# A two-layer RWKV and retention block with routed experts: each scatter and gather of GpSimd tied to an instruction of VectorE, and the scatters moved back

## The chip, the cores and the metric

The kernel runs on one core of a Trainium2 chip. The time is the device time of one execution, in microseconds (us). The engines are TensorE (PE, with its weight loads PEld), VectorE (DVE), ScalarE (ACT), GpSimd (POOL) and SyncE (SP); each takes its instructions in order, and waits at an instruction whose semaphores are not there yet.

## What is computed

The input x is 4 x 1024 tokens of 256 numbers. Two attention layers alternate with the same feed-forward layer, each behind a layer norm and added to x:

```python
x = x + attn_a(layernorm(x))   # RWKV: r, v, k = x @ W; a recurrence over the 1024 tokens; sigmoid(r) * wkv @ W_out
x = x + ffn(layernorm(x))
x = x + attn_b(layernorm(x))   # retention: (q k^T * gamma^(i-j)) v, normed by head, gated, @ wo
x = x + ffn(layernorm(x))

# ffn: 64 experts of 64 hidden units, 4 for each token, and a shared expert for all
_, topk_idx = top_k(x @ router_w + router_bias, 4)
routed = sum over the 4 of score * (silu(x @ wg[e]) * (x @ wu[e])) @ wd[e]
shared = (silu(x @ swg) * (x @ swu)) @ swd
return routed + shared
```

## The kernel before

**Tiling.** The 4096 tokens are cut into 8 segments of 512, numbered 0 to 7, two to a batch row (SPB is 2). A segment is 4 tiles (TT) of 128 tokens. The residual x stays in SBUF for the whole kernel.

**The feed-forward layer** (class `Ffn`, instances f1 and f2) runs in three steps.

- *Route* a segment: norm it (L210, ScalarE, writes the rows `xn_f`), form the router's logits, pick four experts, and count for each token and choice the row `to_f` of a DRAM array `sent` in which it is to lie, so that each expert's tokens stand together in pages of 128 rows. Then *send*: 16 indirect DMAs (L411, issued by GpSimd; 4 tiles x 4 choices) scatter 128 rows each. Beside it runs the *shared* expert: products on TensorE (L435, L448), SiLU on ScalarE (L440), the product with the gate on VectorE (L441), and the sum onto x (L453).
- *Routed* experts: 83 pairs of pages, in order. For each pair SP loads the rows (`rx_f`, L508) and the weights of the pair's experts (`rw_f`, L510); TensorE transposes (L520), VectorE copies (L524, `rxT_f`), TensorE multiplies (L532), ScalarE and VectorE form SiLU and product (L537, L540), TensorE goes down (L551), and ScalarE issues the DMA of the results to a DRAM array `made` (L558). All pages depend on all sends: SP's first load waits until the last one has landed.
- *Gather*: for each tile of 128 tokens, four *fetches* (L580, indirect DMAs of GpSimd) bring its four rows of `made` into a buffer `gy_f`, and four instructions of VectorE (L591) add them onto x, weighted. The adds are due 7 pairs behind the fetches (LAG).

**Order.** Each part of the work is a list of steps. `track(steps, lo, hi)` gives the steps due times spread evenly from lo to hi, and `merge` traces the steps of several tracks by due time. A scheduler then sets the order within each engine; an instruction put under `keep_in_program_order` keeps its place among the others traced. Before the change the adds have this, the sends and fetches do not.

**Stages.** Stage 1 (0 to 385 us) runs the RWKV attention of all eight segments beside the routing and shared expert of f1. The middle (385 to about 1160 us) runs the routed pages and gathers of f1, then stage 2, the retention of four batch rows (`batch(b)`, with the decayed product `pm` at L1009 on VectorE), beside the routing of f2's segments 0 to 5. Its ending routes segments 6 and 7 and runs, as filling, the shared expert of segments 2, 3 and 4 (`fill`, due from 1 to SPB). The second layer (1160 to the end) runs the routed pages, gathers and stores of f2, and the rest of the shared expert.

**Buffers.** The normed rows `xn_f` lie in rotating buffers: 4 in stage 1 (`rows = ffn.rows = (pa, 4)`), 3 in stage 2 (`f2.rows = (pt, 3)`). A norm waits until the sends that read its buffer's earlier contents are done.

Of the kernel before, what the change touches and what calls it, by code (L numbers as in the profile page):

```python
# [10 lines left out]
F32 = mybir.dt.float32  # L11
# [10 lines left out]
P = 128  # L22
D = 256
KC = D // P
SEG = 512
TT = SEG // P
E = 64
F = 64
TOPK = 4
# [19 lines left out]
def track(steps, lo, hi):  # L49

    return [(lo + (hi - lo) * n / len(steps), step) for n, step in enumerate(steps)]
# [9 lines left out]
def hybrid_kernel(ctx: ExitStack, tc: tile.TileContext, a: dict, out: bass.AP):  # L61
    nc = tc.nc
# [10 lines left out]


    USUAL = [(max(E + 2 + 10 * i, (i + 1) * SEG * TOPK // P + E // 2 + 6) + 1) // 2 for i in range(NSEG)]

    def seg_dram(t, i):
        b, s = divmod(i, SPB)
# [148 lines left out]
    class Ffn:  # L227
# [17 lines left out]
        def route(self, i):  # L245
# [159 lines left out]
                nc.vector.tensor_mul(out=wv, in0=wv, in1=bc(sm, 2, TOPK))  # L405
                self.pick[i] = dict(to=to, w=w)

            def send(t):
                for k in range(TOPK):
                    c = t * TOPK + k  # L410
                    ins = nc.gpsimd.indirect_dma_start(  # L411
                        out=rows_sent[: pairs_until(i) * 2 * P, :],
                        out_offset=bass.IndirectOffsetOnAxis(ap=st["to"][:, c : c + 1], axis=0),
                        in_=st["xn"][:, t, :], in_offset=None,
                    )
                    group = f"sends_{self.name}"
                    tc.declare_no_dep(
                        ins.ins, group=group, reason="each token has a row of its own"
                    )
                    tc.add_to_no_dep_group(group, ins.ins)  # L420

            return [norm, logits, pick, rank, place, weigh], [lambda t=t: send(t) for t in range(TT)]

        def shared(self, i):
            nm = f"{self.name}{i}"
            st = {}

            def up(c):
                if c == 0:
                    st["h"] = self.pool.tile([P, NS, SEG], F32, tag="sh", bufs=1, name=f"sh_{nm}")  # L430
                s = slice(c * P, (c + 1) * P)
                g, u = bank("A", f"g_{nm}_{c}"), bank("A", f"u_{nm}_{c}")
                for ps, w in ((g, self.weights[0]), (u, self.weights[1])):
                    for k in range(KC):
                        nc.tensor.matmul(  # L435
                            ps, lhsT=w[:, k, s], rhs=self.xnT[i][:, k, :],
                            start=(k == 0), stop=(k == KC - 1),
                        )
                h = st["h"][:, c, :]
                nc.scalar.activation(out=h, in_=g, func=AF.Silu)  # L440
                nc.vector.tensor_mul(out=h, in0=u, in1=h)  # L441

            def down(q):
                o = bank("C", f"o_{nm}_{q}", [P, 2, D])
                for t in range(2):
                    s = slice((2 * q + t) * P, (2 * q + t + 1) * P)
                    for c in range(NS):
                        nc.tensor.matmul(  # L448
                            o[:, t, :], lhsT=st["h"][:, c, s], rhs=self.weights[2][:, c, :],
                            start=(c == 0), stop=(c == NS - 1),  # L450
                        )
                xt = xs[i][:, 2 * q : 2 * q + 2, :]
                nc.vector.tensor_add(out=xt, in0=o, in1=xt)  # L453

            return [lambda c=c: up(c) for c in range(NS)] + [
                lambda q=q: down(q) for q in range(TT // 2)
            ]
# [38 lines left out]
        def routed(self, pool, until):  # L496
# [18 lines left out]
            def up(p):  # L515
                nm, s = f"{self.name}{p}", st[p]
                tp = bank("B", f"rt_{nm}", [P, KC, 2, P])
                for j in range(2):
                    for k in range(KC):
                        nc.tensor.transpose(  # L520
                            tp[:, k, j, :], s["x"][:, j, k * P : (k + 1) * P], ident
                        )
                xT = pool.tile([P, KC, 2, P], F32, tag="rxT", bufs=2, name=f"rxT_{nm}")
                nc.vector.tensor_copy(out=xT, in_=tp)  # L524
                s["xT"] = xT

            def mid(p):
                nm, s = f"{self.name}{p}", st[p]
                gu = bank("A", f"rg_{nm}", [P, 2, P])
                for j in range(2):  # L530
                    for k in range(KC):
                        nc.tensor.matmul(  # L532
                            gu[:, j, :], lhsT=s["w"][:, j, k * 2 * F : (k + 1) * 2 * F],
                            rhs=s["xT"][:, k, j, :], start=(k == 0), stop=(k == KC - 1),
                        )
                act = pool.tile([P, 2, P], F32, tag="rs", bufs=2, name=f"rs_{nm}")
                nc.scalar.activation(out=act[F:], in_=gu[:F], func=AF.Silu)  # L537

                h = pool.tile([P, 2, P], F32, tag="rh", bufs=2, name=f"rh_{nm}")
                nc.vector.tensor_mul(out=h[:F], in0=gu[F:], in1=act[F:])  # L540
                nc.scalar.copy(out=h[F:], in_=h[:F])  # L541
                s["h"] = h

# [25 lines left out]
        def gather(self, i, pool, until):  # L569


            nm, s = f"{self.name}{i}", self.pick[i]
            ready = [min(until(NSEG - 1), until(i) + PACE * t) for t in range(TT)]
            got = {}

            def fetch(t):
                y = pool.tile([P, TOPK, D], F32, tag="gy", bufs=self.deep[2], name=f"gy_{nm}_{t}")
                for k in range(TOPK):
                    c = t * TOPK + k
                    nc.gpsimd.indirect_dma_start(  # L580
                        out=y[:, k, :], out_offset=None,
                        in_=rows_made[: ready[t] * 2 * P, :],
                        in_offset=bass.IndirectOffsetOnAxis(ap=s["to"][:, c : c + 1], axis=0),
                    )
                got[t] = y

            def add(t):
                for k in range(TOPK):
                    c = t * TOPK + k

                    tc.keep_in_program_order(nc.vector.scalar_tensor_tensor(  # L591
                        out=xs[i][:, t, :], in0=got[t][:, k, :], scalar=s["w"][:, c : c + 1],
                        in1=xs[i][:, t, :], op0=ALU.mult, op1=ALU.add,
                    ))

            return [lambda t=t: fetch(t) for t in range(TT)], [lambda t=t: add(t) for t in range(TT)]

        def gathers(self, pool, until):

# [7 lines left out]

    def stage_1(ctx: ExitStack, ffn, pf):
        pa = ctx.enter_context(tc.tile_pool(name="pa", bufs=1))
        rows = ffn.rows = (pa, 4)  # L610

        rvk = pa.tile([P, KC, 3 * D], F32, name="rvk")
        wout = pa.tile([P, KC, D], F32, name="wout")
# [27 lines left out]
        def wkv(i):  # L641
# [37 lines left out]
            def weights(hf):  # L679
# [9 lines left out]
                    out=o[:, 1:], data0=w_t[:, hf : hf + 1].to_broadcast([P, SEG]), data1=k,  # L689
                    initial=o[:, 0:1], op0=ALU.add, op1=ALU.max,  # L690
                )
                nc.vector.tensor_sub(out=k, in0=k, in1=o[:, :SEG])
                a2, b2, c = (work(n, hf) for n in ("a2", "b2", "c"))
                nc.scalar.activation(out=a2, in_=k, func=AF.Relu, bias=w_neg[:, hf : hf + 1])
                nc.scalar.activation(
# [10 lines left out]
            def sums(hf):  # L706
# [10 lines left out]
                nc.vector.tensor_add(out=den, in0=c, in1=q[:, :SEG])  # L717
                nc.scalar.activation(out=inv, in_=den, func=AF.Ln)
                nc.scalar.activation(out=inv, in_=inv, func=AF.Exp, scale=-1.0)
                nc.vector.tensor_mul(out=b2, in0=b2, in1=v)  # L720
                nc.vector.tensor_tensor_scan(
                    out=p[:, 1:], data0=a2, data1=b2, initial=p[:, 0:1], op0=ALU.mult, op1=ALU.add
                )
                y = pa.tile([P, SEG], F32, tag=f"y{hf}", bufs=2, name=f"y_{i}_{hf}")
                num = a2
                nc.vector.tensor_mul(out=num, in0=c, in1=v)
                nc.vector.tensor_add(out=num, in0=num, in1=p[:, :SEG])
                nc.vector.scalar_tensor_tensor(
                    out=num, in0=s["r"], scalar=1.0, in1=num, op0=ALU.add, op1=ALU.mult
# [2 lines left out]
                nc.vector.scalar_tensor_tensor(  # L732
                    out=inv, in0=den, scalar=2.0, in1=inv, op0=ALU.subtract, op1=ALU.mult
                )
                nc.vector.scalar_tensor_tensor(
                    out=y, in0=num, scalar=-0.5, in1=inv, op0=ALU.mult, op1=ALU.mult
                )
                st[f"y{hf}"] = y

            def output(h):  # L740
# [35 lines left out]
        for i in range(NSEG):  # L776
# [8 lines left out]
            tracks.append(track([lambda f=output, h=h: f(h) for h in range(TT // 2)], at + 1.6, at + 1.7))  # L785
            choose, send = ffn.route(i)
            tracks.append(track(choose, at + 1.8, at + 3.3))
            tracks.append(track(send, at + 3.3, at + 3.4))

            behind = max(0, i - NSEG + 4)  # L790
            tracks.append(track(ffn.shared(i), at + 2.2 + 2 * behind, at + 4.2 + 2 * behind))
# [4 lines left out]
    def stage_2(ctx: ExitStack):  # L796
# [117 lines left out]
        def batch(b):  # L914
# [91 lines left out]

            def decayed(j, g):
                pm = pw.tile([P, KC, 2, CH], F32, tag="pm", bufs=5, name=f"pm_{b}_{j}_{g}")
                nc.vector.tensor_mul(  # L1009
                    out=pm, in0=ch[j]["sc"][g],  # L1010
                    in1=decay.rearrange("p (k g b) n -> p g k b n", k=KC, b=2)[:, g],
                )
                ch[j]["pm"][g] = pm

            def values(j):
# [107 lines left out]
    def first_layer(until):  # L1123
# [14 lines left out]
        with right("turned") as pt:  # L1138
# [13 lines left out]
            beside = [[s for s in batches if s[0] >= cut]]  # L1152
            for i in range(last):
                choose, send = f2.route(i)
                beside.append(track(choose + send, at[i], at[i + 1]))
                if i < BESIDE:
                    beside.append(track(f2.shared(i), at[i + 1], at[i + 3]))
            merge(*beside)
# [3 lines left out]
            for n, i in enumerate(range(last, NSEG)):  # L1162
                choose, send = f2.route(i)
                ending += [
                    track(choose[:2], 0, 0.2), track(choose[2:], n + 0.2, n + 1),
                    track(send, SPB, SPB + 1),
                ]
            fill = []
            for i in range(BESIDE, BESIDE + FILL):
# [89 lines left out]
```

## Time and profile before

| | |
|---|---|
| time, median of 9 runs | 1475.5 us (1472.83 to 1479.4) |
| the profiled execution's own time | 1477.4 us |
| its span | 1475.7 us |
| mean granted clock of TensorE | 0.956 |
| busy: PE, DVE, ACT, POOL | 1279.3, 999.5, 747.6, 518.4 us |
| sends (L411) | 256, mean 1046 ns, from 88.0 to 1166.4 us |
| fetches (L580) | 256, mean 968 ns |

Times of single events are microseconds from the start of the span, in one profiled execution. In a row of the groups stand the line, the engine, the operation, its output and inputs and the count; then busy time and mean ns of one; then the idle time of the engine just before such instructions, and what ended most of it. In a timeline a row is start, duration, engine, line, operation, and in square brackets the idle time ahead of it and what released it. In the list of waits the three numbers are us in all, times, and the longest.

### The profile page before, as it was taken

What the parts mean: (1) busy time and instruction counts of PE and PEld (TensorE: products, weight loads), DVE (VectorE), ACT (ScalarE), POOL (GpSimd) and SP (SyncE); (2) the same over time, 40 slices, a digit from 0 to 9 for tenths busy, and PEclk for the clock granted to TensorE, in tenths of its full rate; (3) what the DMA queues carried; (4) which work ended last, traced back from release to release, by engine and by line L of the source; (5) the groups of instructions that cost most, each with busy time, mean ns of one, the idle gap of its engine ahead of it and who ended that gap; (6) DMA issues with size and microseconds to landing.
All of it is one profiled execution on the core that took longest, in us unless ns stands there. A gap on an engine that the chain in (4) does not pass through costs nothing. (4 is left out here: it accounts for less than half of the span.)

```text
span 1475.7 us, 23662 instructions
## 1 busy us (share of the span) xinstructions
PE 1279.3 (87%) x7872; PEld 897.5 (61%) x7872; DVE 999.5 (68%) x2490; ACT 747.6 (51%) x1433; POOL 518.4 (35%) x536
## 2 busy tenths in 40 slices
PE   6789999999388778999998997999998699998982
PEld 2455545655266666777776664667755477866752
DVE  6998989997255456677767775577659155576654
ACT  7988888953044444557544463254253044444440
POOL 0042344455300244424234105363143400277655
PEclk9999999999699999999999898999999899999997
DMA  9975921113599975666552011121011499999994
GB/s 351 401 229 78 290 93 58 58 54 100 169 323 332 325 254 162 198 204 210 169 169 89 25 48 67 48 92 46 30 58 43 139 318 321 353 389 390 371 316 120
DMA packets 192298, 276.27 MB, mean 187 GB/s; under 512 B 53795, under 2 KB 119718, under 8 KB 192166
## 3 DMA queue, kind: packets, MB, share of 16 engines
q1 hardware_dynamic: 143686, 163.98, 35.0%
q0 software_dynamic: 24576, 67.14, 13.7%
q10 hardware_dynamic: 23904, 43.53, 7.8%
q8 instruction: 65, 1.06, 0.3%
q14 instruction: 67, 0.55, 0.1%
HBM read 166.05 MB, written 121.11 MB: 195 GB/s over the span
## 5 line engine op out<-in xcount | busy, mean ns | idle before, releaser
L411 POOL DMA_INDIRECT sent<-xn_f,to_f x256 | 267.7, 1046 | 463.6 <-issue 217.9
L580 POOL DMA_INDIRECT gy_f<-made,to_f x256 | 247.8, 968 | 481.2 <-DMA made<-ry_f 149.4
L532 PE MATMUL rg_f<-rxT_f,rw_f 128*128 128x128 f32 x1328 | 188.2, 285 | 16.0 <-DVE rxT_f L524 7.4
L532 PEld LDWEIGHTS rg_f<-rxT_f,rw_f 128*128 128x128 f32 x1328 | 166.8, 196 | 28.0 <-DVE rxT_f L524 20.3
L537 ACT ACTIVATE rs_f<-rg_f 64x256 f32<-64x256 f32 x166 | 62.2, 375 | 230.7 <-PE rg_f L532 204.9
L524 DVE COPY rxT_f<-rt_f 128x512 f32<-128x512 f32 x166 | 114.3, 689 | 80.6 <-PE rt_f L520 78.7
L520 PE MATMUL rt_f<-ident,rx_f 128*128 128x128 f32 x664 | 108.1, 286 | 67.4 <-DMA rx_f<-sent 57.8
L551 PE MATMUL rp_f<-rw_f,rh_f 64*128 64x128 f32 x1328 | 133.3, 299 | 4.2 <-DVE rh_f L540 2.1
L591 DVE SCALAR_TENSOR_TENSOR x<-gy_f,w_f,x 128x256 f32<-128x256 f32 x256 | 122.5, 481 | 14.2 <-DMA gy_f<-made,to_f 9.5
L520 PEld LDWEIGHTS rt_f<-ident,rx_f 128*128 128x128 f32 x664 | 74.2, 144 | 94.9 <-issue 47.5
L557 ACT COPY ry_f<-rp_f 128x256 f32<-128x256 f32 x266 | 93.1, 373 | 74.8 <-PE rp_f L551 48.1
L448 PE MATMUL o_f<-f_swd,sh_f 128*128 128x256 f32 x512 | 123.0, 387 | 8.6 <-DVE sh_f L441 4.2
L435 PE MATMUL g_f<-xnT_f,f_swg 128*128 128x512 f32 x256 | 128.2, 616 | 1.3 <-DVE pm L1009 0.8
L435 PE MATMUL u_f<-xnT_f,f_swu 128*128 128x512 f32 x256 | 122.1, 596 | 0.7 <-DVE sh_f L441 0.7
L551 PEld LDWEIGHTS rp_f<-rw_f,rh_f 64*128 64x128 f32 x1328 | 99.4, 188 | 30.6 <-issue 8.4
L448 PEld LDWEIGHTS o_f<-f_swd,sh_f 128*128 128x128 f32 x512 | 95.3, 192 | 30.8 <-issue 6.7
L540 DVE TENSOR_TENSOR rh_f<-rg_f,rs_f 64x256 f32<-64x256 f32 x166 | 70.7, 426 | 63.8 <-ACT rs_f L537 60.8
L1009 DVE TENSOR_TENSOR pm<-sc,decay 128x512 f32<-128x512 f32 x128 | 84.5, 683 | 24.2 <-PE sc L1001 19.2
L655 PE MATMUL rvk<-xnT_a,rvk 128*128 128x512 f32 x192 | 91.2, 621 | 7.9 <-DVE xnT_a L224 7.5
L541 ACT COPY rh_f<-rh_f 64x256 f32<-64x256 f32 x166 | 66.9, 403 | 40.2 <-DVE rh_f L540 31.6
L441 DVE TENSOR_TENSOR sh_f<-u_f,sh_f 128x512 f32<-128x512 f32 x64 | 43.6, 683 | 61.3 <-PE u_f L435 44.5
L440 ACT ACTIVATE sh_f<-g_f 128x512 f32<-128x512 f32 x64 | 37.8, 596 | 89.7 <-PE g_f L435 52.7
(238 smaller groups left out, 2184.3 us busy)
## 6 DMA issues: line engine op xcount, KB each, us to landing
rw_f<-wx SPq DMA_DIRECT2D x332, 192.0 KB
rx_f<-sent SPq DMA_DIRECT2D x166, 256.0 KB
made<-ry_f ACTq DMA_DIRECT2D x166, 256.0 KB
sent<-zeros SPq DMA_DIRECT2D x7, 2048.0 KB
sent<-zeros SPq DMA_DIRECT2D x1, 10240.0 KB
x<-in_x_dram SPq DMA_DIRECT2D x8, 512.0 KB
wx<-in_wg_dram SPq DMA_DIRECT2D x2, 2048.0 KB
sent<-xn_f,to_f POOLq DMA_INDIRECT x256, 2.4
```

The lines of the kernel that those rows point to most:

```text
L411: ins = nc.gpsimd.indirect_dma_start(out=rows_sent[: pairs_until(i) * 2 * P, :], out_offset=bass.IndirectOffsetOnAxis(ap=st["to"][:, c : c ...
L435: nc.tensor.matmul(ps, lhsT=w[:, k, s], rhs=self.xnT[i][:, k, :], start=(k == 0), stop=(k == KC - 1),)
L448: nc.tensor.matmul(o[:, t, :], lhsT=st["h"][:, c, s], rhs=self.weights[2][:, c, :], start=(c == 0), stop=(c == NS - 1),)
L520: nc.tensor.transpose(tp[:, k, j, :], s["x"][:, j, k * P : (k + 1) * P], ident)
L524: nc.vector.tensor_copy(out=xT, in_=tp)
L532: nc.tensor.matmul(gu[:, j, :], lhsT=s["w"][:, j, k * 2 * F : (k + 1) * 2 * F], rhs=s["xT"][:, k, j, :], start=(k == 0), stop=(k == KC - 1),)
L551: nc.tensor.matmul(yp[:, j, :], lhsT=s["h"][r, j, :], rhs=s["w"][r, j, WD:], start=True, stop=True,)
L557: copy(out=y[:, :, c * P : (c + 1) * P], in_=yp)
L580: nc.gpsimd.indirect_dma_start(out=y[:, k, :], out_offset=None, in_=rows_made[: ready[t] * 2 * P, :], in_offset=bass.IndirectOffsetOnAxis( ...
L591: tc.keep_in_program_order(nc.vector.scalar_tensor_tensor(out=xs[i][:, t, :], in0=got[t][:, k, :], scalar=s["w"][:, c : c + 1], in1=xs[i][ ...
L655: nc.tensor.matmul(ps, lhsT=rvk[:, k, lo : lo + P], rhs=st["xnT"][:, k, :], start=(k == 0), stop=(k == KC - 1),)
L1009: nc.vector.tensor_mul(out=pm, in0=ch[j]["sc"][g], in1=decay.rearrange("p (k g b) n -> p g k b n", k=KC, b=2)[:, g],)
```

## The change

A helper `beat` notes the latest of some instructions of VectorE as they are traced: the shared expert's product (L441), the routed copy and product (L524, L540), four steps of the RWKV sums (L692, L720, L726, L735) and the decayed product (L1009). A helper `on_beat` keeps a send or fetch in program order and adds a wait for the beat noted last, if that lies in the same block of the program. All sends and all fetches get it. A segment's sends become 8 steps of two in place of 4 of four, its fetches 16 steps of one in place of 4 of four. Three due times of sends move: in stage 1 from 3.3..3.4 to 3.6..5.4 steps after the segment's, in stage 2 behind the choice by one segment's time, in the ending from SPB..SPB + 1 to SPB + n/2..SPB + n/2 + 0.5 (n is 0 for segment 6 and 1 for segment 7). In stage 1 the rows get five buffers.

```diff
+    beats = {}
+
+    def beat(ins):
+
+        beats.update(name=ins.ins.name, bb=nc.cur_bb)
+
+    def on_beat(ins):
+
+        tc.keep_in_program_order(ins)
+        if beats.get("bb") is nc.cur_bb:
+            tc.add_manual_dep(
+                ins.ins, beats["name"],
+                mybir.DependencyInfo(mybir.DependencyClass.Sync, mybir.DependencyReason.DATA),
+                reason="on_beat",
+            )
...
-            def send(t):
-                for k in range(TOPK):
+            def send(t, half):
+                for k in range(half * TOPK // 2, (half + 1) * TOPK // 2):
...
+                    on_beat(ins)
+
+            return [norm, logits, pick, rank, place, weigh], [
+                lambda t=t, h=h: send(t, h) for t in range(TT) for h in range(2)
+            ]
...
-                nc.vector.tensor_mul(out=h, in0=u, in1=h)
+                beat(nc.vector.tensor_mul(out=h, in0=u, in1=h))
...
+            def fetch(t, k):
+                if k == 0:
+                    got[t] = pool.tile(
+                        [P, TOPK, D], F32, tag="gy", bufs=self.deep[2], name=f"gy_{nm}_{t}"
+                    )
+                c = t * TOPK + k
+                ins = nc.gpsimd.indirect_dma_start(
+                    out=got[t][:, k, :], out_offset=None,
+                    in_=rows_made[: ready[t] * 2 * P, :],
+                    in_offset=bass.IndirectOffsetOnAxis(ap=s["to"][:, c : c + 1], axis=0),
+                )
+                on_beat(ins)
...
-        rows = ffn.rows = (pa, 4)
+        rows = ffn.rows = (pa, 5)
...
-            tracks.append(track(send, at + 3.3, at + 3.4))
+            tracks.append(track(send, at + 3.6, at + 5.4))
...
-                beside.append(track(choose + send, at[i], at[i + 1]))
+                beside.append(track(choose, at[i], at[i + 1]))
+                beside.append(track(send, at[i + 1] + 0.5, 2 * at[i + 1] - at[i] + 0.5))
...
-                    track(send, SPB, SPB + 1),
+                    track(send, SPB + n / 2, SPB + n / 2 + 0.5),
```

## The prediction

> **What bounds the kernel now.** I read the page first, for busy shares and the costliest groups, then the waits of each engine, then the timelines of GpSimd, VectorE, ScalarE and TensorE around the places where a send or fetch ends a wait.
>
> ```profile
> span 1475.7 us, 23662 instructions
> ...
> PE 1279.3 (87%) x7872; PEld 897.5 (61%) x7872; DVE 999.5 (68%) x2490; ACT 747.6 (51%) x1433; POOL 518.4 (35%) x536
> ...
> L411 POOL DMA_INDIRECT sent<-xn_f,to_f x256 | 267.7, 1046 | 463.6 <-issue 217.9
> L580 POOL DMA_INDIRECT gy_f<-made,to_f x256 | 247.8, 968 | 481.2 <-DMA made<-ry_f 149.4
> ```
>
> TensorE is busy 87% and is the bound in the middle; the second layer runs with the DMA engines busy 0.96 to 1.05 of the time. GpSimd is busy 35%: its sends and fetches cost time only where another engine waits for them. The page's groups give the unit: a send takes 1.05 us, a fetch 0.97, and the timeline shows 0.30 idle between two, so 32 sends in a row need 41 us. The waits of each engine hold two places where sends end a long idle time: SP's first load of the second layer's routed rows, and one norm on ScalarE.
>
> (The columns are us in total, times, longest.)
>
> ```profile
> SPq L508 <- DMA sent<-xn_f,to_f: 37.3, 1, 37.3
> ```
>
> ```profile
> ACT xn_f L210 <- DMA sent<-xn_f,to_f: 17.9, 1, 17.9
> ```
>
> The boundary before the second layer, in GpSimd's timeline and then VectorE's:
>
> ```profile
> 1094.52 0.96 POOL L411 DMA_INDIRECT sent<-xn_f,to_f  x1 [0.30 <-issue]
> 1126.33 1.10 POOL L411 DMA_INDIRECT sent<-xn_f,to_f  x1 [30.86 <-ACT w_f L401]
> 1127.73 0.96 POOL L411 DMA_INDIRECT sent<-xn_f,to_f  x1 [0.30 <-issue]
> ...
> 1166.41 0.96 POOL L411 DMA_INDIRECT sent<-xn_f,to_f  x1 [0.30 <-issue]
> ```
>
> ```profile
> 1145.39 0.69 DVE L441 TENSOR_TENSOR sh_f<-u_f,sh_f 128x512 f32<-128x512 f32 x1 [2.25 <-PE u_f L435]
> 1148.83 0.69 DVE L441 TENSOR_TENSOR sh_f<-u_f,sh_f 128x512 f32<-128x512 f32 x1 [2.74 <-PE u_f L435]
> 1152.21 0.69 DVE L453 TENSOR_TENSOR x<-o_f,x 128x512 f32<-128x512 f32 x1 [2.69 <-PE o_f L448]
> 1156.72 0.69 DVE L453 TENSOR_TENSOR x<-o_f,x 128x512 f32<-128x512 f32 x1 [3.81 <-PE o_f L448]
> 1160.25 0.69 DVE L441 TENSOR_TENSOR sh_f<-u_f,sh_f 128x512 f32<-128x512 f32 x1 [2.84 <-PE u_f L435]
> 1172.75 0.69 DVE L524 COPY rxT_f<-rt_f 128x512 f32<-128x512 f32 x1 [11.81 <-PE rt_f L520]
> ```
>
> The last 32 sends (segments 6 and 7) run from 1126.33 to 1167.4 without a gap, beside the shared expert of segment 4 (the 'fill'). They begin as soon as segment 6's destinations exist; nothing orders them against the fill. The fill ends, VectorE goes idle for 11.81 us, and the first routed page follows the last send. So here **the sends are the path**: what delays the first of them delays the kernel.
>
> **The change, part by part.**
>
> *The ending's sends.* Due times put the last 32 sends half a step behind all of the fill, and each now waits for the last beat traced ahead of it. In the built order that beat is, for all 32, the fill's last product, the row at 1148.83, ending at 1149.52. VectorE's last 70 instructions of this stage stand in the same order in both programs, and so do TensorE's, SP's and GpSimd's of the whole second layer, so nothing fills the hole. A send starts 0.7 to 0.8 us after what it waited for (segment 6's destinations were done at 1125.6, the send began at 1126.33), so the first starts at 1150.3: 24.0 later. Queued behind it on GpSimd are the other 31, behind those on SP the page loads of the whole layer, whose first load of rows waits for all of them, and behind that TensorE. The stream loses a few lengthened sends (1.10, 1.49, 1.14 in this row of 32), at most 0.9 us, as VectorE and TensorE are idle under its second half. **+23.3** (22.5 to 24.0).
>
> *Sends of segments 0 to 5 of the second layer*, one segment later. The one wait of ScalarE above is norm L210 of segment 3, whose buffer (3 in rotation) still holds segment 0's rows:
>
> ```profile
> 885.54 0.60 ACT L440 ACTIVATE sh_f<-g_f 128x512 f32<-128x512 f32 x1
> 904.06 0.60 ACT L210 ACTIVATE xn_f<-x,off_f,rstd_f 128x256 f32<-128x256 f32 x1 [17.92 <-DMA sent<-xn_f,to_f]
> ```
>
> ScalarE stands still from 886.14 to 904.06, TensorE runs dry 10.7 us later (896.8) and idles 8.18 us, with 2.3 us more in short gaps after it: 10.5 us lost. In the changed order that norm stands some 20 ScalarE instructions later, behind two more products of segment 0's shared expert, which ScalarE reaches at 929.4 by the clock of before. Segment 0's last sends wait for beats at 925.4 (a decayed product, L1009) and 927.8 (L441); eight are queued behind the first: 8 x 1.265 = 10.1 us, and 2.4 to land, from 925.4 + 0.7, so 938 at the latest. ScalarE waits about 8 us in place of 17.9, and TensorE lasted 10.7 us before. By that row the loss goes entirely (-10.5); if the cover is thinner there, all of it stays (0). I take **-7**, nearer to the full gain, as 8 is under 10.7. The next two such norms have their buffers at 974 (needed 984.6) and 994 (needed 1000): no stall, but the second has 6 us only; if sends slip by 10, it costs 4. Segment 5's sends now end near 1101 and not 1095.5, ahead of segment 6's at 1126: free.
>
> *Sends of the first layer.* Segments 0 to 4 move up to 20 us later (segment 0 from 105 to 124). Their readers are the buffers, now five: the next use of segment 0's has about 65 us of slack. The last three segments' sends are set by their own destinations, and their beats are long past:
>
> ```profile
> 362.14 1.31 POOL L411 DMA_INDIRECT sent<-xn_f,to_f  x1 [5.46 <-ACT w_f L401]
> ...
> 382.89 0.96 POOL L411 DMA_INDIRECT sent<-xn_f,to_f  x1 [0.30 <-DMA sent<-xn_f,to_f]
> ```
>
> The order of all five engines in this block is the same. The last send of this layer stays where it is: **0** (-1 to +1).
>
> *Fetches of the first layer* (501 to 817). Most beats lie at or before the fetch's present start. The late ones are late by 5 to 12 us: segment 3's second group from 606-610 to 613-620, segment 5's first from 691.7 to 704.4, its third from 722.1 to 733.3, segment 6's second from 757.5 to 768, its last from 785.3 to 794.6. Behind them on GpSimd wait only other fetches; VectorE's adds (L591) come later: 653.7, 733.3, 765.3, 797.6, 803.8. The tightest is the last: 794.6 + 0.8 + 0.96 and 4.8 to land is 801.2, 2.6 us ahead. The last segment's 16 fetches keep their times. **0** (0 to +4: the tightest group late by all of its landing).
>
> *Fetches of the second layer.* Each beat lies 0.9 to 8 us before the fetch's present start, and GpSimd runs them back to back. In the tail (1443 to 1467) the beats are at or before 1443.1, the first fetch at 1447.7. A second condition may cost a wait instruction of 17 ns (the shortest of GpSimd's in the trace): 16 x 0.017 = **+0.3** (0 to 1).
>
> *Contention.* A reason for beats would be that a transfer is described faster in VectorE's shadow. Sends above the usual 0.96 us add up to 256 x 0.086 = 22 us, all GpSimd's, and of these under 1 us lies at each boundary. VectorE pays nothing: L441 took 0.69 us beside a send and without one. The Trainium skill (SBUF — State Buffer, "Who interferes with whom") says that GpSimd can't write descriptors while VectorE holds the shared port in a two-port mode, so a transfer of 620 ns can take 3100. The trace agrees in kind (minimum 954 ns, longest 4488) but not in weight: the median is 960. By the rule's ratio freeing the sends would gain hundreds of us; by the rows the path gains 1 at most.
>
> **Sum:** 23.3 - 7 + 0.3 = +16.6. On the profiled execution's own time, 1477.4 (its span 1475.7 and 1.7 around it), 1494.0; that execution lies 1.9 above the median of nine, 1475.5, so on the median **1492**.
>
> **The rivals.**
>
> *Stage 2 chokes as well* (0.12). The pacing holds rows longer, three buffers turn over one segment later, and ScalarE's wait comes back at segments 3, 4 and 5. For it: the 6 us margin above. Against: a later need as well. Price: the 10.5 stay and up to 10 are added: 23.3 + 0 to 10, 1499 to 1509.
>
> *Faster* (0.07). ScalarE's stall goes whole (-10.5) and the boundary is covered: this needs the 32 sends to start no later than about 1126 + 10, that is the fill done 14 us sooner than it now is. For it: with the stall gone the chain into the fill might move ahead of segment 6's routing. Against: the fill's order behind the routing is the same on VectorE. It decides from a boundary loss under 10.5; full price 1475.5 - 10.5 = 1465.
>
> *The change does not bind* (0.04). Beats already past at most places, and a stall gain cancelling part of the boundary: 1472 to 1479. Against: for 32 sends the beat is 23 us away.
>
> **How the numbers follow.** My forecast (1485 to 1498) has 0.77, the choking 0.12, faster 0.07, no effect 0.04. The range takes the sum's ends, 1475.5 + 22.5 - 10.5 = 1487 with some room below, and the choking's lower half: 1482 to 1505. About 0.2%, 3 us, is what a measurement can tell from no change; so faster 0.07, same 0.04, slower 0.89.
>
> **What would show it.** GpSimd's timeline: the first of the last 32 sends about 24 us behind segment 6's destinations and under 1 us behind the fill's last product; VectorE's gap before the first L524 copy of the second layer at about 35 us and not 11.81; SP's wait for sends longer by about 23; ScalarE's longest wait at L210 under 10 us, and TensorE without the 8.18 gap. I am wrong if the second layer begins at its old distance from the routing, if L210 still waits 18, or if adds (L591) wait for fetches between 650 and 810.

## The result, and the profile after

| | before | after |
|---|---|---|
| median | 1478.31 us (62 runs) | 1494.05 us (20 runs) |
| ratio of after to before, 95% interval | | 1.0112, 1.0098 to 1.0127 |
| the profiled execution, span | 1475.7 us | 1498.3 us |
| granted clock of TensorE in it | 0.956 | 0.943 |

The change makes the kernel 1.12% slower, 16.6 us of 1478.31 (14.5 to 18.8 by the interval; the medians themselves lie 15.7 apart). The profiled spans lie 22.6 us apart; why that is more than 16.6 is said below, with the length of the second layer. Lines of the changed kernel are numbered anew: the send is L427, the fetch L601, the shared product L460, the routed copy L543, the norm L226. The kernels of the experiments have numbers of their own; the names tell which instruction a row is (`sh_f` on VectorE the shared product, `rxT_f` the routed copy, `xn_f` on ScalarE the norm).

The page of the changed kernel, the span and the two groups of GpSimd:

```profile
span 1498.3 us, 23758 instructions
...
L427 POOL DMA_INDIRECT sent<-xn_f,to_f x256 | 272.3, 1064 | 475.6 <-issue 179.9
L601 POOL DMA_INDIRECT gy_f<-made,to_f x256 | 249.8, 976 | 485.1 <-DMA made<-ry_f 128.1
```

A send did not get shorter (1046 ns before, 1064 after), nor a fetch. The loss is at the boundary before the second layer. GpSimd's timeline there (start, duration, then the idle time ahead and its releaser), and VectorE's:

```profile
1093.38 0.96 POOL L427 DMA_INDIRECT sent<-xn_f,to_f  x1 [0.30 <-issue]
1141.87 0.95 POOL L427 DMA_INDIRECT sent<-xn_f,to_f  x1 [47.53 <-DVE sh_f L460]
1143.13 0.96 POOL L427 DMA_INDIRECT sent<-xn_f,to_f  x1 [0.30 <-issue]
...
1181.03 0.96 POOL L427 DMA_INDIRECT sent<-xn_f,to_f  x1 [0.30 <-issue]
```

```profile
1117.50 0.16 DVE L409 TENSOR_TENSOR to_f<-to_f,to_pg_f 128x16 uint32<-128x16 uint32 x1
...
1140.91 0.69 DVE L460 TENSOR_TENSOR sh_f<-u_f,sh_f 128x512 f32<-128x512 f32 x1 [2.74 <-PE u_f L454]
...
1152.33 0.69 DVE L460 TENSOR_TENSOR sh_f<-u_f,sh_f 128x512 f32<-128x512 f32 x1 [2.84 <-PE u_f L454]
1187.38 0.69 DVE L543 COPY rxT_f<-rt_f 128x512 f32<-128x512 f32 x1 [34.37 <-PE rt_f L539]
```

The first of the last 32 sends names the product as its releaser: GpSimd was idle 47.53 us, and segment 6's destinations (`to_f`, the first row of VectorE) had been done at 1117.7. The row at 1140.91 is the fill's last product, that at 1152.33 the first of segment 5. The hole ahead of the first routed copy is 34.37 us and was 11.81. From the fill's last product to that copy it takes 46.5 us and took 23.9: **+22.6**. SP's wait for sends grew from 37.3 to 60.1:

```profile
SPq L527 <- DMA sent<-xn_f,to_f: 60.1, 1, 60.1
```

The product itself comes 7.9 us sooner than before (1140.91 for 1148.83). Of these, 1.8 lie ahead of the first layer's last routed copy (776.14 for 777.92), and 6.1 in stage 2, where ScalarE waits less. ScalarE's timeline, with the one row that answers to the wait of 17.92:

```profile
908.94 0.60 ACT L459 ACTIVATE sh_f<-g_f 128x512 f32<-128x512 f32 x1 [2.84 <-PE g_f L454]
916.13 2.07 ACT L226 ACTIVATE xn_f<-x,off_f,rstd_f 128x256 f32<-128x256 f32 x4 [6.59 <-DMA sent<-xn_f,to_f]
```

### The profile page after: what moved, and what is told of

The parts are those of the page before. It is cut to its first block, busy times and chain, and to the rows that moved or that the text cites. A ratio compares the mean times of both kernels' runs of the same rounds, so it can differ in the third digit from the quotient of the medians.

```text
span 1498.3 us, 23758 instructions
## 1 busy us (share of the span) xinstructions
PE 1291.0 (86%) x7872; PEld 910.9 (61%) x7872; DVE 1000.5 (67%) x2491; ACT 745.5 (50%) x1431; POOL 525.1 (35%) x536
## 5 line engine op out<-in xcount | busy, mean ns | idle before, releaser
L427 POOL DMA_INDIRECT sent<-xn_f,to_f x256 | 272.3, 1064 | 475.6 <-issue 179.9
L601 POOL DMA_INDIRECT gy_f<-made,to_f x256 | 249.8, 976 | 485.1 <-DMA made<-ry_f 128.1
L543 DVE COPY rxT_f<-rt_f 128x512 f32<-128x512 f32 x166 | 114.3, 689 | 86.3 <-PE rt_f L539 84.2
L570 PE MATMUL rp_f<-rw_f,rh_f 64*128 64x128 f32 x1328 | 139.6, 302 | 5.1 <-DVE rh_f L559 3.3
L467 PE MATMUL o_f<-f_swd,sh_f 128*128 128x256 f32 x512 | 128.7, 400 | 8.7 <-DVE sh_f L460 4.5
L570 PEld LDWEIGHTS rp_f<-rw_f,rh_f 64*128 64x128 f32 x1328 | 105.5, 191 | 32.2 <-ACT ry_f L576 8.0
L467 PEld LDWEIGHTS o_f<-f_swd,sh_f 128*128 128x128 f32 x512 | 99.0, 199 | 33.7 <-issue 8.3
L1032 DVE TENSOR_TENSOR pm<-sc,decay 128x512 f32<-128x512 f32 x128 | 84.4, 683 | 22.6 <-PE sc L1024 19.2
L454 PEld LDWEIGHTS u_f<-xnT_f,f_swu 128*128 128x128 f32 x256 | 48.2, 191 | 56.9 <-issue 51.8
```

The lines of the kernel that those rows point to most:

```text
L427: ins = nc.gpsimd.indirect_dma_start(out=rows_sent[: pairs_until(i) * 2 * P, :], out_offset=bass.IndirectOffsetOnAxis(ap=st["to"][:, c : c ...
L454: nc.tensor.matmul(ps, lhsT=w[:, k, s], rhs=self.xnT[i][:, k, :], start=(k == 0), stop=(k == KC - 1),)
L467: nc.tensor.matmul(o[:, t, :], lhsT=st["h"][:, c, s], rhs=self.weights[2][:, c, :], start=(c == 0), stop=(c == NS - 1),)
L543: beat(nc.vector.tensor_copy(out=xT, in_=tp))
L570: nc.tensor.matmul(yp[:, j, :], lhsT=s["h"][r, j, :], rhs=s["w"][r, j, WD:], start=True, stop=True,)
L601: ins = nc.gpsimd.indirect_dma_start(out=got[t][:, k, :], out_offset=None, in_=rows_made[: ready[t] * 2 * P, :], in_offset=bass.IndirectOf ...
```

## The experiments

Two theories were set against each other. **Mine:** the boundary costs 23 us and the later norm of stage 2 gives back about 7; everything else is free. **The rival:** the waits cost something in many places (fetches, tail, stage 2), and the boundary is partly covered by the 12 us hole that was there. The ratios of the experiments are to the kernel before, in runs beside it on one chip.

### The last sends freed

```diff
-                    on_beat(ins)
+                    if not (self.name == "f2_" and i >= NSEG - SPB):
+                        on_beat(ins)
...
-                    track(send, SPB + n / 2, SPB + n / 2 + 0.5),
+                    track(send, SPB, SPB + 1),
```

> The changed kernel, but the last 32 sends (segments 6 and 7 of the second layer) neither kept in program order nor made to wait for a beat, and due as before. The order of the instructions on all five engines is that of the changed kernel; only this wait is gone. Theory (the boundary is the loss, stage 2 is a gain): the first of the 32 sends starts at segment 6's destinations again, VectorE's gap before the first routed copy of the second layer is about 12 us in place of 34, the time falls by 22 to 24 us below the changed kernel and ends 5 to 8 us below the kernel before. Rival (the paced sends and fetches cost time as well): it stays at or above the kernel before, ratio 1.000 to 1.006.

Measured: 1472.68 us, ratio 0.9963 (0.9940 to 0.9987). GpSimd's timeline of this kernel, then VectorE's:

```profile
1118.75 1.10 POOL L427 DMA_INDIRECT sent<-xn_f,to_f  x1 [24.06 <-ACT w_f L417]
```

```profile
1141.25 0.69 DVE L461 TENSOR_TENSOR sh_f<-u_f,sh_f 128x512 f32<-128x512 f32 x1 [2.74 <-PE u_f L455]
...
1165.26 0.69 DVE L544 COPY rxT_f<-rt_f 128x512 f32<-128x512 f32 x1 [11.89 <-PE rt_f L540]
```

The first send starts at the destinations again, the hole is 11.89, and from product to copy it takes 24.0 us as before. All other waits of the change are still in this kernel, and it is faster than the one before by 0.37%, 5.5 us. So the rest of the change is a gain, and the boundary is the loss.

### The last sends alone held back

The helpers `beat` and `on_beat` are those of the change; due times and everything else are as in the kernel before.

```diff
+                    if (self.name == "f2_" and i >= NSEG - SPB):
+                        on_beat(ins)
...
-                nc.vector.tensor_mul(out=h, in0=u, in1=h)
+                beat(nc.vector.tensor_mul(out=h, in0=u, in1=h))
```

> The kernel before, with one part of the change: the last 32 sends wait for the last product of the filling shared expert (L441). Order on PE, DVE, ACT and SP as in the kernel before. Theory: the boundary alone costs 22 to 24 us, ratio 1.015 to 1.016, VectorE's gap before the first routed copy near 35 us, and ScalarE's wait of 17.9 us in stage 2 is still there. Rival (the second layer also runs slower in the changed kernel for another reason, such as the fetches' waits): the boundary costs clearly less than the change and the gain of stage 2 together, ratio under 1.012.

Measured: 1502.52 us, ratio 1.0156 (1.0125 to 1.0187), that is 23.1 us of 1477.7. ScalarE's wait of 17.9 us is still there. VectorE's timeline:

```profile
1148.36 0.69 DVE L459 TENSOR_TENSOR sh_f<-u_f,sh_f 128x512 f32<-128x512 f32 x1 [2.74 <-PE u_f L453]
...
1194.73 0.69 DVE L542 COPY rxT_f<-rt_f 128x512 f32<-128x512 f32 x1 [34.26 <-PE rt_f L538]
```

The hole is that of the changed kernel (34.26), the product is where it was before (1148.36). One part of the change, in the kernel before, makes the whole loss.

### The last sends held back half as long

The beat is now only the first of the four products of segment 4's shared expert.

```diff
-                beat(nc.vector.tensor_mul(out=h, in0=u, in1=h))
+                ins = nc.vector.tensor_mul(out=h, in0=u, in1=h)
+                if i == BESIDE + FILL - 1 and c == 0:
+                    beat(ins)
```

> The kernel before, with the last 32 sends waiting for the first of the four products of the filling segment 4 (near 1139.2 to 1139.9 us) in place of its last (1148.8). Theory (the sends are the path from the moment segment 6's destinations exist, so each us of delay is a us lost): first send at 1140.6, 14.3 later than before, less up to 0.9 for fewer lengthened sends: +13 to +14.5 us, ratio 1.009 to 1.010. Rival (the 12 us in which VectorE is idle before the second layer are slack that covers a delay of that size): +0 to +3 us, ratio 1.000 to 1.002.

Measured: 1492.99 us, ratio 1.0105 (1.0080 to 1.0130), 15.5 us with 11.8 to 19.2 in the interval. GpSimd's and VectorE's timelines:

```profile
1139.40 0.96 POOL L427 DMA_INDIRECT sent<-xn_f,to_f  x1 [47.05 <-DVE w_f L416]
```

```profile
1138.45 0.68 DVE L459 TENSOR_TENSOR sh_f<-u_f,sh_f 128x512 f32<-128x512 f32 x1
...
1184.95 0.69 DVE L544 COPY rxT_f<-rt_f 128x512 f32<-128x512 f32 x1 [24.58 <-PE rt_f L540]
```

The beat, the product at 1138.45, ends at 1139.13; the send names a small instruction of VectorE that ends just behind it. The first send is 13.1 us later than before (1126.33), the hole 12.8 us longer (24.58 for 11.81). The old hole covers nothing of a delay: it was itself made by the sends, not by slack beside them.

### The fetches freed

```diff
                     in_offset=bass.IndirectOffsetOnAxis(ap=s["to"][:, c : c + 1], axis=0),
                 )
-                on_beat(ins)
```

> The changed kernel without the beats on the fetches, so that only sends wait. Theory: the fetches' waits cost nothing, the time is that of the changed kernel within 0.2%, ratio to the kernel before 1.010 to 1.013. Rival (pacing the fetches delays adds and the stores in the tail): 3 to 8 us faster than the changed kernel, ratio 1.005 to 1.009.

Measured: 1495.76 us, ratio 1.0117 (1.0087 to 1.0148): as the changed kernel. The waits of 256 fetches cost nothing that can be measured; the interval is 0.3% wide to each side.

### Four buffers for stage 2's rows, and the same once more

```diff
-            f2.rows = (pt, 3)
+            f2.rows = (pt, 4)
```

> The kernel before with four buffers in place of three for the normed rows of stage 2, so that segment 3's norm does not wait for segment 0's sends; nothing else is changed by hand. Theory (that wait of 17.9 us costs 7 to 10 us of TensorE): TensorE's gap of 8 us near 900 is gone and the time falls by 6 to 10 us, ratio 0.993 to 0.996. Rival (the time returns later, as the boundary or the DMA engines are late anyway): ratio 0.998 to 1.001.

> The kernel before with four buffers once more, on the same chip as the two versions above, to compare them, and for a second profile of the same program: how far do two executions of one program lie apart in the second layer? Theory (the second layer's length varies by several us from execution to execution, the stages ahead of it by under 1 us): ratio 0.990 to 0.994, fill's last product within 1 us of 1136.0, second layer between 300 and 311 us. Rival (each program has a second layer of its own length): 309 us again within 1 us.

Measured: 1467.21 us, ratio 0.9916 (0.9883 to 0.9950); again, on another chip, 1463.44 us, 0.9890 (0.9866 to 0.9915). The second ratio is a little under the 0.990 to 0.994 expected. ScalarE waits for no send in stage 2. VectorE's timeline in the first of the two:

```profile
1136.00 0.69 DVE L441 TENSOR_TENSOR sh_f<-u_f,sh_f 128x512 f32<-128x512 f32 x1 [2.74 <-PE u_f L435]
...
1160.03 0.69 DVE L524 COPY rxT_f<-rt_f 128x512 f32<-128x512 f32 x1 [11.92 <-PE rt_f L520]
```

The fill's last product comes at 1136.00 and 1135.81, about 13 us sooner than before, more than the 6 to 10 expected and more than the 10.5 us of TensorE's idle time that the prediction took for all of this wait's price. The second layer, from its first routed copy to the end, took 309.1 us in the one execution and 303.6 in the other, of one program: the length of that part is not a property of the program to better than 5 us. The kernel before was profiled at 302.9, the changed one at 310.9, so 8 of the 22.6 us between the spans lie in this part. In the ten other executions with the same work there it took 302.6 to 310.2; those with the fetches' waits (302.6 to 310.9) and those without (302.9 to 310.2) are not apart. So these 8 us are within the spread, and no cost of the change is seen in them.

### Only the due times of stage 2, without beats

```diff
-                beside.append(track(choose + send, at[i], at[i + 1]))
+                beside.append(track(choose, at[i], at[i + 1]))
+                beside.append(track(send, at[i + 1] + 0.5, 2 * at[i + 1] - at[i] + 0.5))
```

> The kernel before, with only the due times of stage 2's sends moved back by one segment; no beats, nothing kept in program order, the ending as before. It tells whether the gain in stage 2 comes from the order of the work or from the waits for beats. Theory (order: segment 3's norm stands later on ScalarE, and the beats only hold the sends up): without beats segment 0's rows come free earlier, ScalarE's wait is under the 6.6 us of the changed kernel, the fill's last product comes 7 to 12 us earlier than before, ratio 0.991 to 0.996. Rival (the beats place the sends where they do less harm): the gain is lost, ratio 0.998 to 1.002.

Measured: 1477.08 us, ratio 0.9996 (0.9976 to 1.0015). My theory fell here: the due times alone bring no gain. ScalarE still waits 13.88 us, TensorE idles 12.6 us:

```profile
907.71 0.60 ACT L210 ACTIVATE xn_f<-x,off_f,rstd_f 128x256 f32<-128x256 f32 x1 [13.88 <-DMA sent<-xn_f,to_f]
```

### Program order alone, without the waits

```diff
         tc.keep_in_program_order(ins)
-        if beats.get("bb") is nc.cur_bb:
-            tc.add_manual_dep(
-                ins.ins, beats["name"],
-                mybir.DependencyInfo(mybir.DependencyClass.Sync, mybir.DependencyReason.DATA),
-                reason="on_beat",
-            )
```

> The changed kernel without any wait for a beat: the sends and fetches keep their place in program order, split and spread as in the change, and nothing more. In the built order segment 3's norm then stands at place 618 of ScalarE's instructions of this stage, where it is 616 in the kernel before and 639 in the changed one. Theory (it is the wait for the beat, as the scheduler counts it, that moves this norm behind other work, and that holds the last 32 sends up): neither the gain nor the loss is there; ScalarE waits 13 to 18 us for sends, the first of the last 32 sends starts at segment 6's destinations, ratio 0.998 to 1.001. Rival (program order and spreading alone make the change): ratio 1.005 to 1.013 if they hold up the boundary, under 0.997 if they bring stage 2's gain.

Measured: 1476.22 us, ratio 0.9983 (0.9963 to 1.0002). ScalarE's timeline:

```profile
888.86 0.60 ACT L453 ACTIVATE sh_f<-g_f 128x512 f32<-128x512 f32 x1
903.39 0.60 ACT L220 ACTIVATE xn_f<-x,off_f,rstd_f 128x256 f32<-128x256 f32 x1 [13.93 <-DMA sent<-xn_f,to_f]
```

Neither gain nor loss is left, and ScalarE waits 13.93 us. From the first layer's last routed copy to the fill's last product this kernel takes 370.0 us, the kernel before 370.9, the one with the last sends freed 364.9. So both gain and loss come from the waits for beats. In stage 2 they do it by way of the scheduler: with them segment 3's norm stands at place 639 of ScalarE's instructions of this stage, without them at 618, before at 616; with the due times alone it also stands two places behind that of before. The sends themselves go out later with the beats (segment 0's last at 913.6, before at 901.5), which by itself would lengthen the wait, but ScalarE has other work until then. That the place does it is argued from this; no run has the later place without the waits.

### Four buffers in the changed kernel

The edit is that of four buffers, in the changed kernel.

> The changed kernel with four buffers for the normed rows of stage 2 in place of three. Theory (the changed kernel still loses some 5 us to ScalarE's remaining wait of 6.6 us): the wait is gone, the fill's last product moves from 1140.9 to about 1136, the boundary still takes its 46 us from that product to the first routed copy, and the time is 4 to 6 us under the changed kernel, ratio to the kernel before 1.006 to 1.009. Rival (the remaining wait is covered): as the changed kernel, 1.010 to 1.013.

Measured: 1481.80 us, ratio 1.0029 (1.0004 to 1.0055). That is about 0.8% under the changed kernel's 1.0112, 12 us, where 4 to 6 were expected. Of the changed kernel's two remaining waits (6.59 and 2.65 us) only the first is gone; the second, at segment 4's norm, is still there (2.65 us at 966.34). The first thus cost more than its own length. The trace shows how. TensorE's timeline around its gap, in the changed kernel:

```profile
914.86 0.69 PE L1024 MATMUL sc<-qx,kT 32*128 32x256 f32 x2
918.72 0.69 PE L275 MATMUL lp_f<-wr_sb,xnT_f 128*128 128x64 f32 x2 [3.17 <-ACT xnT_f L240]
...
935.43 0.38 PE L319 MATMUL rk_f<-room_f,first_row 128*128 128x320 bf16 x1
```

The same instructions with four buffers:

```profile
908.64 0.69 PE L1024 MATMUL sc<-qx,kT 32*128 32x256 f32 x2
909.26 0.43 PE L275 MATMUL lp_f<-wr_sb,xnT_f 128*128 128x64 f32 x2
...
917.98 0.30 PE L319 MATMUL rk_f<-room_f,first_row 128*128 128x320 bf16 x1
```

From the first to the last of these rows it is 20.6 us in the one kernel and 9.3 in the other: 11.2 us more for the same work, of which the gap is 3.17. TensorE's busy time and granted clock in stretches of 4 us (the number behind the stretch is its length; then busy time and count of PE, PEld, DVE, ACT and POOL; then the granted clock, the DMA share and GB/s), in the changed kernel:

```profile
916.00:920.00 4.00, 1.28 (x4) 1.19 (x5) 0.00 (x0) 2.54 (x5) 0.00 (x0) 0.81 0.00 0
920.00:924.00 4.00, 4.00 (x17) 3.40 (x16) 0.30 (x1) 0.37 (x1) 0.00 (x0) 0.50 0.00 0
924.00:928.00 4.00, 4.00 (x11) 2.34 (x10) 3.32 (x17) 0.00 (x0) 1.31 (x2) 0.50 0.05 15
928.00:932.00 4.00, 4.00 (x9) 2.68 (x9) 1.34 (x3) 0.00 (x0) 1.46 (x1) 0.50 0.16 54
932.00:936.00 4.00, 4.00 (x14) 3.00 (x13) 0.32 (x1) 0.00 (x0) 0.00 (x0) 0.55 0.00 0
936.00:940.00 4.00, 4.00 (x51) 2.70 (x49) 3.62 (x11) 0.86 (x2) 0.07 (x1) 1.00 0.00 0
```

ScalarE's wait left TensorE idle for 3.17 us before 918.72, and then TensorE ran at half its clock until about 936, busy all the time: some 17 us at 0.50, so about 8 us of work lost. Idle and slow clock together make the 11.2 us, near the 12 by which the time fell. (In the profiled executions stage 2, from the first layer's last routed copy to the fill's last product, is 9.0 us shorter, 355.7 for 364.8; and this execution of the kernel with four buffers is one of its fastest, 1475.53 us, with a median of 1481.80.) With four buffers the clock reads 1.00 in all of these stretches. In the kernel before, the same stretches behind its gap of 8.18 us:

```profile
904.00:908.00 4.00, 2.18 (x6) 1.41 (x7) 1.09 (x4) 3.94 (x10) 0.00 (x0) 0.50 0.00 0
908.00:912.00 4.00, 4.00 (x11) 3.03 (x10) 3.97 (x8) 2.41 (x5) 0.00 (x0) 0.53 0.00 0
912.00:916.00 4.00, 4.00 (x31) 2.95 (x30) 2.62 (x12) 3.35 (x6) 0.52 (x1) 1.00 0.01 4
```

A longer gap, but the clock was back at 1.00 by 912, about 7 us after TensorE began again at 904.97.

### The versions that beat both kernels

The two corrections together: last sends free, four buffers, the rest as in the change.

> The changed kernel with the last 32 sends free (as in the first experiment) and four buffers for stage 2's rows. Theory (the two corrections add): stage 2 is 15 to 16 us shorter than in the kernel before, as with four buffers in the changed kernel, the boundary costs nothing, ratio 0.988 to 0.992. Rival (without the waits of the ending the kernel has no more to gain than four buffers alone give, since the DMAs of the second layer set the end): 0.991 to 0.994.

Measured: 1457.90 us, ratio 0.9857 (0.9833 to 0.9880), the fastest of all. The boundary in VectorE's timeline:

```profile
1126.04 0.69 DVE L461 TENSOR_TENSOR sh_f<-u_f,sh_f 128x512 f32<-128x512 f32 x1 [2.74 <-PE u_f L455]
...
1137.46 0.69 DVE L461 TENSOR_TENSOR sh_f<-u_f,sh_f 128x512 f32<-128x512 f32 x1 [2.84 <-PE u_f L455]
1149.91 0.69 DVE L544 COPY rxT_f<-rt_f 128x512 f32<-128x512 f32 x1 [11.76 <-PE rt_f L540]
```

The hole is the old one, and the copy comes 22.8 us sooner than before (1172.75). From the first layer's last routed copy to the fill's last product this kernel takes 354.7 us, the one before 370.9: 16.2 us, about as expected. The ratio is lower than the 0.988 to 0.992 of the expectation: another 6.6 us lie ahead of that, 4.2 of them in stage 1 of this execution, of which more below; how much of the ratio is chance of that kind stays open. On the same chip, four buffers alone gave 0.9890 (0.9866 to 0.9915); the two intervals overlap, so the lead over that version is not settled.

The hole of 12 us invites filling, with the shared expert of a fourth segment; first with four buffers alone, then in the version above.

```diff
-    BESIDE, FILL = 2, 3
+    BESIDE, FILL = 2, 4
```

> The kernel before with four buffers for stage 2's normed rows, and a fourth segment's shared expert taken out of the second layer into the hole ahead of it, which was 12.6 us of VectorE with three. It looks for a version better than four buffers alone. Theory (the hole is free room): 3 to 10 us under four buffers alone, ratio 0.985 to 0.990. Rival (a segment's shared expert takes some 20 us of TensorE, more than the hole, and the second layer is bound by its DMAs, so taking work out of it gains nothing): as four buffers alone or up to 8 us slower, ratio 0.992 to 0.997.

> As the version with the last sends free and four buffers, and a fourth segment's shared expert in the hole ahead of the second layer. Theory (taking work of TensorE out of the second layer gains nothing, as with four buffers alone): the same as that version within 0.3%. Rival (with stage 2 shorter the hole is worth filling): 4 to 8 us less.

Measured: 0.9945 (0.9919 to 0.9971) and 0.9896 (0.9866 to 0.9926), each above its version without the edit (0.9916, 0.9857), with intervals that overlap. The hole is gone (the routed copy follows the product before it at once, 1161.15 for 1160.55), but that copy comes no sooner than with three segments (1160.03 with four buffers alone; in the second pair 1159.20 for 1149.91, of which 5.6 us come from stage 1). The second layer took 299.6 and 306.7 us with less work in it, 303.6 to 309.1 and 307.0 without the edit: work taken out of it was not worth any time there that could be told from the spread of 5 us and more.

## Why the prediction was right, and where its steps were not

- **The ending's sends, +23.3.** Right in place, price and mechanism. The sends alone held back cost 23.1 us; the trace of the changed kernel has 22.6. The half-long delay (first send 13.1 us later, hole 12.8 us longer, time 15.5 us with an interval of 11.8 to 19.2) shows that the old hole covers none of it. One term was off by half a us: the send began 0.27 us behind the product (1141.87 for 1141.60), where 0.7 to 0.8 was taken.
- **Sends of stage 2, -7.** The sum was right: with the ending undone the kernel gains 5.5 us (1.9 to 8.9 by the interval). The working under it was not. It set ScalarE's remaining wait at about 8 us, where its own terms, 925.4 + 0.7 + 10.1 + 2.4, give 938.6 and so 9.2 (6.59 measured), and held this to be covered by the 10.7 us that TensorE lasted before. TensorE lasted only 6.0 us (ScalarE stood still from 909.54, TensorE from 915.55), was idle for 3.17 us, and then ran some 17 us at half clock. And it capped the wait's price at 10.5 us of idle time, with nothing for the clock; taking the wait away in the kernel before gave 12.4 us (ratio 0.9916 of 1477.7) and 16.3 (0.9890 of 1480.07), in the two profiles 11.7 and 13.1 us of stage 2. The 8 us gap there also drew about 7 us at half clock. The cap was too low and the share won too high, and the two errors met.
- **The cause in stage 2** was put on the segment's later due times, as one edit with the beats. It is the beats: due times alone, and order alone, give nothing (0.9996, 0.9983).
- **Fetches, 0.** Right: without their waits 1.0117, with them 1.0112.
- **The first layer's sends, 0.** Right: the first routed copy comes at 397.7 us, before at 397.4, though segment 0's sends now wait and pause.
- **The tail, +0.3**, is under what these runs resolve.
- **Contention, at most 1 us of gain.** Right: the mean of a send went up by 18 ns, and the longest took 4488 ns in both kernels. (On the page that the prediction names, the 620 and 3100 ns stand in the section "A bandwidth-pool intuition that's wrong (but worth ruling out)".)
- **Choking** did occur in a small form, a second wait of 2.65 us at segment 4's norm, for which the prediction saw 10 us of room (974 for 984.6), and the fill still came 7.9 us sooner. **Faster** failed at its own condition: the hole gave no cover. **Not binding** failed too: the waits bind, as the kernel without them, at 0.9983, shows.

The prediction's 16.6 us are the measured 16.6 (14.5 to 18.8); by the errors named, a part of that closeness is luck.

The Trainium skill (TensorE: Matmul & The Clock Gate, "Part 1: The HAM clock gate") has the array fall to half clock after an idle window of about 3.4 us, and return to full after about 3.4 us of sustained work. The first part comes near the half clock seen behind the 3.17 us gap, though that gap is a little shorter than the page's window. The second does not agree: in the changed kernel the half clock lasted some 17 us of unbroken work. The page's own figure would make the clock's loss 1.7 us (an estimate: half of 3.4), where the trace has about 8.

## What to carry to other kernels

When a transfer is tied to another engine's progress, look at which of the tied transfers stands last before a barrier: here the waits of 256 fetches were free, and the wait of the last 32 sends cost its full length, as everything was behind it; and an idle hole next to it is no slack if that transfer made the hole. A short stall of TensorE costs more than its length when the clock follows it down (here 11.2 us for a gap of 3.17), so one more buffer, which removed the wait, beat the pacing that only shortened it (0.9916 and 0.9890 against 0.9963). And before an effect in a scheduled program is put to a due time, compare the built orders: here the wait acted through where the scheduler put another engine's instruction.

## What the runs showed of the hardware that was not expected

- A gap of 3.17 us on TensorE was followed by some 17 us at a granted clock of 0.50 under full load, and so in all three executions that have this gap (the changed kernel, the last sends freed, the fetches freed); behind gaps of 8.1 to 8.2 us (three executions) and 12.6 us (two) the clock was back 3.5 to 7.8 us after TensorE began again. What sets the length was not tried.
- Stage 1 in the same order took 397 to 399 us to the first routed copy in most profiled executions, but 392.4, 393.2 and 396.1 in three (four buffers in the changed kernel, the fastest version, program order alone). In these three the clock read 1.00 from 80 to 120 us, in the eleven others, the changed kernel among them, 0.91. Whether that is chance or goes with the program stays open.
- The second layer's length varies by 5 us between two executions of one program and by 8 over the twelve executions in which TensorE, VectorE, ScalarE and GpSimd have the same work there in the same order. Its cause was not sought.
